# Two attention blocks on one core: where the softmax sums are inverted, and when the next job's sums are formed

## The chip, the cores and the metric

The kernel runs on one core of one Trainium2 chip. The metric is the time of one execution on the device in microseconds (us).

## The reference

The input x has 8 images of 512 channels and 32 x 32 positions (S = 1024 tokens). Two layers follow each other. Each normalises x in 8 groups of channels, projects it to q, k and v (1 x 1 convolutions, 512 to 512 each), runs attention with 8 heads of 64 channels, projects the output and adds x:

```python
xn = ((xg - mean) * jax.lax.rsqrt(var + EPS)).reshape(B, C, H, W)
...
qkv = jnp.einsum('oc,bchw->bohw', qkv_w, xn) + qkv_b[None, :, None, None]
...
attn = jax.nn.softmax(jnp.einsum('bhds,bhdt->bhst', q, k) * scale, axis=-1)
out = jnp.einsum('bhst,bhdt->bhds', attn, v).reshape(B, C, H, W)
return x + jnp.einsum('oc,bchw->bohw', proj_w, out) + proj_b[None, :, None, None]
```

## The kernel before, in words

**Jobs.** The work is cut into 16 jobs, one for an image and a layer, in the order (image 0, layer 0), (image 1, layer 0), (image 0, layer 1), (image 1, layer 1), then the next two images. For each job there are products for v, k and q and the attention. The output projection of job n is done together with the projections of job n+1. All four projections are done with Strassen-like products: seven products of half blocks in place of eight, in most cases over two levels. The sums and differences of blocks that these need are made on VectorE: `sums` (line 1295, tiles `t` and `xn`) and `deep_steps` (tile `deep`, lines 482 to 488) for the next job's normalised input, `out_combine` (line 452 for part 0) for this job's output, `factor` (lines 162 to 168) for the weights.

**Attention.** A job's attention has 8 groups (4 pairs of heads, 2 halves of the queries) of 8 steps each, so 64 steps numbered i = 0 to 63, with i up to 65 to drain. In each step TensorE makes scores `sc` (line 1099), ScalarE takes the exponential into an `e` tile (line 1104), and two steps later TensorE multiplies it with v into `po` (line 1150). The sums over keys are formed beside this: in the first four steps of a group, two `e` tiles are added by a DMA that accumulates (issued by POOL, line 1127) and the sum is added on VectorE five steps later (line 1130); in the last four steps VectorE adds them (lines 1118 and 1120). The `e` tiles come from a pool of twelve, which also holds the weights `w` fetched for the next products. At the end of a group `take` copies half of `po` on ScalarE (`px`, line 1171) and adds the other half on VectorE (line 1173), and `reduce` sums `acc` over its rows into `r` (line 1185).

**The part that is moved.** After every second group, `reduce` sets up four small functions: `gather` (three `r<-r` DMAs on SP, line 1208), `invert` (sum `lt` line 1212, reciprocal line 1213, transposes line 1224, one DMA `rd<-rt` line 1225 and two `rb<-rd` line 1227), `spread` (only in the last pair of groups, line 1236) and `normalise` (a multiplication of two groups' output by `rb`, line 1242). They are put on a clock that the kernel keeps while it is being written out: each attention step advances it by 1.71 us, each end of a group by another 0.85, each step of a projection by its own amount. `later(delay, fn)` puts `fn` at clock + delay, and `advance` emits what has come due. So `times` are planned delays; they set where in VectorE's instruction order a function stands, and the engines then follow the order and their waits.

**Chores and moves.** The other work beside an attention is put at step numbers by hand. `put(i, fn)` places a chore at step i or the next free one, `move(i, fn)` does the same for loads and stores. Among them are the statistics of the next job's input, `groups` and `factors` of its normalisation (lines 331 to 338 and 349 to 351; `factors` needs `mr`, which comes by a DMA, line 341), four `apply` on ScalarE (line 356), the four `sums`, the `deep_steps` and `out_combine`. In jobs 0 to 3 (`ROUNDS`) there is also a "round": a weight is loaded into a tile with the tag `deep`, its factors are formed and seven blocks are stored (`deep<-round`, line 235). In jobs 0 and 1 (`FIRST`) a raw weight is loaded by `put_first` (`raw`, line 157), its factors are formed and stored (`keep<-raw`, line 173). Round, raw weight and deep sums share one buffer, since the tag `deep` has one.

**Order.** TensorE, ScalarE and VectorE run in the order in which the program is written out (`manual_schedule`). The order on SP and POOL is chosen by the planner of the language, by program position and by what it takes to be ready; in the profile the stores of a round stand on SP well ahead of the step at which they are written.

**The end.** The last job has no next one. Its groups go by halves of the queries, and after it `last_proj` makes the output projection in two halves; `put5` (line 1058) and `put` (line 1064) add to x, and the sums for the second half (`last_sums(1)`, lines 1018 to 1027) are placed on the clock from 7.1 us after the attention.

Of the kernel before, what the change touches and what calls it, by code (L numbers as in the profile page):

```python
# [54 lines left out]
ROUNDS = {0: (O, 0), 1: (V, 1), 2: (O, 1), 3: (V, 0)}  # L55
# [26 lines left out]
def fast_path(  # L82
# [33 lines left out]
    def later(delay, fn):  # L116
        todo.append((clock[0] + delay, fn))
# [36 lines left out]
    def load_blocks(w, layer, which):  # L154
        for i in range(2):
            for j in range(2):
                nc.sync.dma_start(w[:, 2 * j + i], raw_block(layer, which, i, j))
# [12 lines left out]
    def store_factors(w, layer, which):  # L170
        keep = wdram.tile([P, NW, 2, CH], F32, name=f"keep_{which}_{layer}")
        for s in (slice(S1, NW), slice(S3, S3 + 1)):
            nc.sync.dma_start(keep[:, s], w[:, s])
        factors[which, layer] = keep
# [272 lines left out]
    def out_combine(src, t, part):  # L447

        b11, b12 = src[:, 0:2, :HALF], src[:, 0:2, HALF:]
        b21, b22 = src[:, 2:4, :HALF], src[:, 2:4, HALF:]  # L450
        if part == 0:
            nc.vector.tensor_sub(b12, b12, b11)
        elif part == 1:
            nc.vector.tensor_sub(t[:, 1], b22, b12)
        elif part == 2:
            nc.vector.tensor_sub(t[:, 0], t[:, 1], b11)
        else:
            nc.vector.tensor_sub(t[:, 2], b21, t[:, 1])
# [619 lines left out]
    class Attention:  # L1078
# [101 lines left out]
        def reduce(self, g):  # L1180
            n, q, m = self.n, self.q, g % 2
            hp, sh = self.groups[g]
            if m == 0:
                self.r = small.tile([P, NQ, 2, RP], F32, tag="r", name=f"r_{n}_{g}", bufs=1)
            nc.vector.tensor_reduce(  # L1185
                self.r[:, 0, m, :], self.acc.pop(g).rearrange("p j (b e) -> p (j b) e", e=RP), AX.X,
                ALU.add, apply_transpose=True,
            )
            if m == 0:
                return  # L1190
            before = self.groups[g - 1]
            if before[0] == hp:
                place = q[:, hp, :].rearrange("p (m e) -> p m e", m=2)
            else:
                place = q[:, hp - 1 : hp + 1, sh * HALF : (sh + 1) * HALF]
            r, first = self.r, slice(0, RP)
            ends = g + 1 == len(self.groups)
            lt = small.tile([RP, 2, RP], F32, tag="lt", name=f"lt_{n}_{g}", bufs=1)
            ri = small.tile([P, 2, 2, RP // 2], F32, tag="ri", name=f"ri_{n}_{g}", bufs=1)
            box = []  # L1200

            def gather():
                for i in range(1, NQ):
                    src, to_ = r[i * RP : (i + 1) * RP, 0], r[first, i]
                    if ends:
                        nc.vector.tensor_copy(to_, src)
                    else:
                        nc.sync.dma_start(to_, src)

            def invert():  # L1210
                inv = ri[first].rearrange("p m j b -> p m (j b)")
                nc.vector.tensor_reduce(lt, r[first].rearrange("p a m b -> p m b a"), AX.X, ALU.add)
                nc.vector.reciprocal(inv, lt)
                box.append(apool.tile([P, 2, HALF], F32, tag="rb", name=f"rb_{n}_{g}", bufs=1))
                if ends:
                    for i in range(1, NQ):
                        nc.vector.tensor_copy(
                            ri[i * RP : (i + 1) * RP, :, 0, :], ri[first, :, i * RP // HD, :]
                        )
                else:  # L1220
                    rt = small.tile([RP, 2, RP], F32, tag="rt", name=f"rt_{n}_{g}", bufs=1)
                    rd = dram.tile([2, 2, HALF], F32, tag="rd", name=f"rd_{n}_{g}")
                    for i in range(2):
                        nc.vector.transpose(rt[:, i, :], inv[:, i, :])
                    nc.sync.dma_start(rd.rearrange("m j (b e) -> (j b) m e", e=RP), rt)
                    for j in range(2):
                        nc.sync.dma_start(
                            box[0][j * HD : (j + 1) * HD],
                            rd[:, j, :].unsqueeze(0).to_broadcast([HD, 2, HALF]),
                        )  # L1230
                nc.vector.tensor_max(lmax, lmax, lt)
                nc.vector.tensor_max(rmax, rmax, inv)

            def spread():
                if ends:
                    nc.vector.transpose(
                        box[0].rearrange("p m (b e) -> p m b e", e=RP),
                        ri[:, :, 0, :].unsqueeze(3).to_broadcast([P, 2, RP // 2, RP]),
                    )

            def normalise():
                nc.vector.tensor_mul(place, place, box[0])
                whole[0] = n if ends else -1

            times = (0.0, 7.6, 7.7, 16.2)
            if ends:
                times = (0.0, 0.2, 7.6, 8.2) if n + 1 >= DEEP_V else (0.0, 0.2, 2.0, 4.0)
                if n + 1 == len(jobs):
                    times = (0.0, 0.2, 2.0, 7.0)
            for at, step in zip(times, (gather, invert, spread, normalise)):  # L1250
                later(at, step)

# [287 lines left out]
    for n in range(-1, len(jobs)):  # L1540
        last = n + 1 == len(jobs)
        outs = None
        if n >= 0:
            chores, moves = {}, {}

            def put(i, fn):
                while i in chores:
                    i += 1
                chores[i] = fn
                return i  # L1550

            def move(i, fn):
                while i in moves:
                    i += 1
                moves[i] = fn
                return i
# [12 lines left out]
                    at = move(at + 1 + i % 2, fn)  # L1569

            def put_first(which, layer):
                at = move(37 if n == 0 else 3, lambda: start()) + 3
                box = []

                def start():
                    box.append(acts.tile([P, NW, 2, CH], F32, tag="deep", name=f"raw_{n}"))
                    load_blocks(box[0], layer, which)

                for part in range(4):
                    at = put(at + 1, lambda part=part: factor(box[0], part))  # L1580
                move(at + 1, lambda: store_factors(box[0], layer, which))

            if last:
                w = last_weights(n)
                for part in range(4):
                    put(12 + 2 * part, lambda part=part: factor(w, part))
                for i, fn in enumerate(last_sums(0)):
                    put(49 + 3 * i, fn)
            else:
                for i, (_, fn) in enumerate(extra):  # L1590
                    put(2 + i, fn)
                if n == 1:
                    at = (8, 14, 15, 16, 18, 19, 21, 24, 27, 30)
                else:
                    for i, fn in zip((3, 3, 4, 5, 5, 6, 7, 7, 8), reads):
                        put(i, fn)
                    at = (16, 22, 23, 24, 26, 27, 29, 31, 33, 35)
                    if n < DEEP_V + 2:
                        at = (17, 23, 24, 25, 27, 28, 30, 32, 34, 36)
                for i, fn in zip(at, steps):  # L1600
                    put(i, fn)
                if n == 1:
                    put_first(*FIRST[n])
                if n in ROUNDS:
                    put_round(*ROUNDS[n])
                if n == 0:
                    put_first(*FIRST[n])
                for i, fn in zip(at[len(steps) :], sums(n + 1)):
                    put(i, fn)
                put(48, lambda q=att.q: out_combine(q, None, 0))  # L1610
                deep_first = deep_steps(n + 1)
                if n + 1 >= DEEP_V:
                    for i, fn in enumerate(deep_first):
                        put((42 if n in ROUNDS else 37) + 2 * i, fn)
                else:
                    for at, fn in zip((50, 52, 54, 56), deep_first[4:]):
                        put(at, fn)
                move(58, lambda: extend_plan(n + 1))
                for _ in range(RING):
                    move(58, fetch)  # L1620
            assert max([*chores, *moves], default=0) < NT * len(att.groups) + LEAD
            if n + 1 >= DEEP_V and not last:
# [17 lines left out]
                att = Attention(n + 1)  # L1640
# [40 lines left out]
        att = Attention(n + 1)  # L1681
# [253 lines left out]
```

## Time and profile before

| | |
|---|---|
| Time, median of 3 runs (lowest to highest) | 3183.94 us (3182.21 to 3186.64) |
| The profiled execution's own time | 3187.94 us |
| Its span in the profile | 3186.2 us |
| Mean granted TensorE clock | 0.996 |
| Busy: TensorE / VectorE / ScalarE / GpSimd | 3156.2 / 2637.2 / 2333.5 / 281.0 us |
| VectorE's waits at L1212 (`lt`, for `r<-r`) | 23.8 us, 20 times |
| VectorE's waits at L1242 (`q`, for `rb<-rd`) | 22.1 us, 11 times |

PE is TensorE's matrix product, PEld its load of weights, DVE VectorE, ACT ScalarE, POOL GpSimd, and SP the engine that issues most transfers. A name such as `lt<-r` gives what an instruction writes and reads. Busy time is the union of an engine's instructions; sequencer work, such as waiting and issuing transfers, is not in it. A number in brackets after an instruction is the engine's idle time ahead of it, and the arrow names what ended it. The ends of TensorE's products are modelled, so a busy TensorE isn't one at its peak; its holes are the part that can be read with certainty.

### The profile page before, as it was taken

What the parts mean: (1) busy time and instruction counts of PE and PEld (TensorE: products, weight loads), DVE (VectorE), ACT (ScalarE), POOL (GpSimd) and SP (SyncE); (2) the same over time, 40 slices, a digit from 0 to 9 for tenths busy, and PEclk for the clock granted to TensorE, in tenths of its full rate; (3) what the DMA queues carried; (4) which work ended last, traced back from release to release, by engine and by line L of the source; (5) the groups of instructions that cost most, each with busy time, mean ns of one, the idle gap of its engine ahead of it and who ended that gap; (6) DMA issues with size and microseconds to landing.
All of it is one profiled execution on the core that took longest, in us unless ns stands there. A gap on an engine that the chain in (4) does not pass through costs nothing.

```text
span 3186.2 us, 62139 instructions
## 1 busy us (share of the span) xinstructions
PE 3156.2 (99%) x24093; PEld 1872.4 (59%) x24093; DVE 2637.2 (83%) x3571; ACT 2333.5 (73%) x4233; POOL 281.0 (9%) x318
## 2 busy tenths in 40 slices
PE   9999999999999999999999999999999999999998
PEld 8357384573846638466393754837557375573844
DVE  8797898978879788797978969889697887978867
ACT  6648687786877868777686776867768687686863
POOL 0101101011010010100001000010000100001000
PEclk9999999999999999999999999999999999999999
DMA  7645675565745455355554545446456463544633
GB/s 276 141 124 160 153 210 140 147 192 128 213 98 146 119 110 167 75 151 159 144 184 88 159 98 138 125 94 181 131 137 182 89 201 63 136 121 96 220 78 78
DMA packets 186190, 450.31 MB, mean 141 GB/s; under 512 B 37928, under 2 KB 54176, under 8 KB 185888
## 3 DMA queue, kind: packets, MB, share of 16 engines
q1 hardware_dynamic: 137040, 296.82, 27.4%
q0 software_dynamic: 48848, 149.44, 25.8%
q8 instruction: 192, 3.15, 0.4%
q14 instruction: 110, 0.90, 0.1%
HBM read 247.41 MB, written 48.17 MB: 93 GB/s over the span
## 4 chain that ended last, share of the span: by engine, by line
PE 81%; DVE 1%; issue 0%; DMA 0%; ACT 0%; SPq 0%; POOL 0%; DVEq 0%; ACTq 0%; POOLq 0%
PE sc L1099 23%; PE po L1150 23%; PE zd L806 9%; PE vd L806 9%; PE yd L806 4%; PE ud L806 4%; PE vd L801 4%; PE zd L801 3%; PE yd L801 1%; PE ud L801 1%; DVE acc L1120 0%; PE z_last L1042 0%; DMA r<-r 0%; ACT e L1104 0%; DVE x L1064 0%
## 5 line engine op out<-in xcount | busy, mean ns | idle before, releaser
L1104 ACT ACTIVATE e<-sc 128x1024 f32<-128x1024 f32 x1024 | 1043.8, 1025 | 575.6 <-PE sc L1099 546.9
L1099 PE MATMUL sc<-q,k 64*64 64x512 f32 x8192 | 1059.2, 590 | 10.1 <-ACT e L1104 10.1
L1150 PE MATMUL po<-e,v 64*64 64x512 f32 x8192 | 1058.0, 590 | 3.4 <-ACT e L1104 3.4
L1099 PEld LDWEIGHTS sc<-q,k 64*64 64x64 f32 x8192 | 309.6, 133 | 576.7 <-issue 509.9
L1150 PEld LDWEIGHTS po<-e,v 64*64 64x64 f32 x8192 | 311.6, 133 | 572.6 <-issue 544.2
L1120 DVE TENSOR_TENSOR acc<-acc,e 128x1024 f32<-128x1024 f32 x320 | 389.4, 1217 | 39.1 <-ACT e L1104 28.9
L1127 POOL DMA_DIRECT2D e<-e x224 | 192.9, 861 | 1769.0 <-ACT e L1104 1267.8
L1118 DVE TENSOR_TENSOR acc<-e,e 128x1024 f32<-128x1024 f32 x128 | 156.4, 1222 | 147.1 <-ACT e L1104 147.1
L1130 DVE TENSOR_TENSOR acc<-acc,e 128x1024 f32<-128x1024 f32 x224 | 272.4, 1216 | 1.9
L806 PE MATMUL zd<-deep,w 128*128 128x256 f32 x860 | 240.2, 379 | 0.0
L806 PE MATMUL vd<-deep,w 128*128 128x256 f32 x804 | 223.4, 379 | 0.0
L806 PEld LDWEIGHTS zd<-deep,w 128*128 128x128 f32 x860 | 163.3, 190 | 22.5 <-ACT ud L501 0.3
L806 PEld LDWEIGHTS vd<-deep,w 128*128 128x128 f32 x804 | 152.8, 190 | 20.8
L1185 DVE TRANSPOSE_TENSOR_REDUCE r<-acc 128x32 f32<-128x1024 f32 x128 | 159.4, 1245 | 4.3
L901 POOL DMA_DIRECT2D x<-p x61 | 72.9, 1195 | 972.9 <-ACT p L823 453.9
L848 DVE TENSOR_TENSOR p<-p,s 128x512 f32<-128x512 f32 x185 | 127.2, 687 | 22.8 <-ACT p L823 19.3
L801 PE MATMUL vd<-w,deep 128*128 128x128 f32 x840 | 119.1, 275 | 1.1 <-ACT ud L501 1.1
L848 DVE TENSOR_TENSOR q<-q,s 128x512 f32<-128x512 f32 x64 | 44.1, 690 | 86.8 <-ACT q L825 45.1
L801 PE MATMUL zd<-w,deep 128*128 128x128 f32 x728 | 106.5, 275 | 0.9 <-ACT ud L501 0.9
L801 PEld LDWEIGHTS vd<-w,deep 128*128 128x128 f32 x840 | 106.2, 192 | 1.3 <-ACT ud L501 1.3
L806 PE MATMUL vd<-os,w 128*128 128x256 f32 x364 | 105.5, 379 | 0.0
L806 PE MATMUL zd<-os,w 128*128 128x256 f32 x356 | 98.9, 379 | 0.0
(296 smaller groups left out, 4826.4 us busy)
## 6 DMA issues: line engine op xcount, KB each, us to landing
w<-deep SPq DMA_DIRECT2D x399, 448.0 KB, 5.4
e<-e POOLq DMA_DIRECT2D x224, 512.0 KB, 4.7
x<-p POOLq DMA_DIRECT2D x61, 512.0 KB, 6.6
rb<-rd SPq DMA_DIRECT2D x96, 256.0 KB, 3.7
x<-x_dram SPq DMA_DIRECT2D x28, 512.0 KB, 3.7
out_dram<-x SPq DMA_DIRECT2D x28, 512.0 KB, 6.0
deep<-w SPq DMA_DIRECT2D x28, 448.0 KB, 2.7
deep<-round SPq DMA_DIRECT2D x28, 448.0 KB, 4.9
```

What stands on the lines that cost most here:

```text
L801: nc.tensor.matmul(ps[:, tokens], moving[i][:, tokens], lhs[:, FACTOR[i], :], start=(start and ti == 0), stop=True, skip_group_check=True,)
L806: nc.tensor.matmul(ps, lhs[:, FACTOR[i], :], moving[i], start=start, stop=True, skip_group_check=True,)
L848: nc.vector.tensor_add(to_, to_, five.to_broadcast([P, 2, QT]))
L901: nc.gpsimd.dma_start(to_, p(part), accum_op=ALU.add)
L1099: nc.tensor.matmul(sc[h * HD : (h + 1) * HD, j, :], k[r, hp, k0 : k0 + HD], q[r, hp, sh * HALF : (sh + 1) * HALF], start=True, stop=True,)
L1104: nc.scalar.activation(e, sc, AF.Exp, scale=SCALE)
L1118: nc.vector.tensor_add(acc[g], self.es[i - 1], e)
L1120: nc.vector.tensor_add(acc[g], acc[g], e)
L1127: nc.gpsimd.dma_start(self.summed[i], self.summed.pop(i - 1), accum_op=ALU.add)
L1130: nc.vector.tensor_add(self.acc[g], self.acc[g], self.summed.pop(i))
L1150: nc.tensor.matmul(po[g][j * HD : (j + 1) * HD, h, :], v[r, kc, d0 : d0 + HD], e[r, j, :], start=(kc == 0), stop=(kc == NT - 1),)
L1185: nc.vector.tensor_reduce(self.r[:, 0, m, :], self.acc.pop(g).rearrange("p j (b e) -> p (j b) e", e=RP), AX.X, ALU.add, apply_transpose=True,)
```

## The change

In jobs 0 to 3 and groups 0 to 3, the planned delays of `invert` and `normalise` go from 7.6 to 12.0 and from 16.2 to 22.0 us. In the last pair of groups of the last job, `normalise` goes from 7.0 to 9.6. In job 0 the load of the raw weight is asked for at move 31 instead of 37, and by the rule for taken slots stands at 33 (37 before); the four factors follow at steps 37 to 40 (41 to 44 before) and the store at 41 (45 before). Part 0 of `out_combine` goes from step 48 to 52 in jobs 0 to 3. The eight deep sums of jobs 1 to 3 go from 42, 44, 46, 49, 50, 52, 54, 56 to 39, 40, 41, 43, 45, 47, 49, 50; the four of job 0 from 50, 52, 54, 56 to 46 to 49. All other jobs keep their places.

```diff
-            times = (0.0, 7.6, 7.7, 16.2)
+            times = (0.0, 12.0, 12.1, 22.0) if n in ROUNDS and g < 4 else (0.0, 7.6, 7.7, 16.2)
             if ends:
                 times = (0.0, 0.2, 7.6, 8.2) if n + 1 >= DEEP_V else (0.0, 0.2, 2.0, 4.0)
                 if n + 1 == len(jobs):
-                    times = (0.0, 0.2, 2.0, 7.0)
+                    times = (0.0, 0.2, 2.0, 9.6)
...
             def put_first(which, layer):
-                at = move(37 if n == 0 else 3, lambda: start()) + 3
+                at = move(31 if n == 0 else 3, lambda: start()) + 3
...
-                put(48, lambda q=att.q: out_combine(q, None, 0))
+                put(52 if n in ROUNDS else 48, lambda q=att.q: out_combine(q, None, 0))
                 deep_first = deep_steps(n + 1)
                 if n + 1 >= DEEP_V:
                     for i, fn in enumerate(deep_first):
-                        put((42 if n in ROUNDS else 37) + 2 * i, fn)
+                        put(37 + 2 * i if n not in ROUNDS else (39, 40, 41, 43, 45, 47, 49, 50)[i], fn)
                 else:
-                    for at, fn in zip((50, 52, 54, 56), deep_first[4:]):
+                    for at, fn in zip((46, 47, 48, 49), deep_first[4:]):
                         put(at, fn)
```

## The prediction

> **What bounds it now.** I read the engines' shares first, then busy time in 50 us stretches, then the waits and the timeline around each TensorE hole.
>
> ```profile
> PE 3156.2 (99%) x24093; PEld 1872.4 (59%) x24093; DVE 2637.2 (83%) x3571; ACT 2333.5 (73%) x4233; POOL 281.0 (9%) x318
> ...
> 100.00:150.00 50.00, 46.64 (x424) 15.87 (x420) 28.72 (x42) 32.20 (x34) 7.89 (x9) 0.97 0.72 171
> 150.00:200.00 50.00, 46.40 (x427) 15.58 (x420) 46.28 (x55) 28.62 (x30) 3.94 (x5) 1.00 0.49 115
> ...
> 500.00:550.00 50.00, 46.42 (x432) 16.17 (x428) 40.44 (x56) 32.66 (x35) 7.43 (x8) 1.00 0.64 156
> ...
> 700.00:750.00 50.00, 46.81 (x424) 16.15 (x420) 40.41 (x56) 32.36 (x34) 7.42 (x8) 0.97 0.63 152
> ...
> 900.00:950.00 50.00, 50.00 (x472) 17.74 (x468) 39.23 (x53) 35.71 (x38) 6.57 (x8) 1.00 0.48 93
> ```
>
> The columns are stretch, length, then PE, PEld, DVE, ACT and POOL busy. TensorE sets the pace and is full nearly everywhere; no work on it is removed. Only its holes can be won, 3186.2 − 3156.2 = 30 us in all, and about 7 of those are the last output's way out. The holes lie in jobs 0 to 3, the jobs that the change touches. In job 3:
>
> ```profile
> 730.38 1.22 DVE L1120 TENSOR_TENSOR acc<-acc,e 128x1024 f32<-128x1024 f32 x1
> 733.54 0.59 DVE L1212 TENSOR_REDUCE lt<-r 32x64 f32<-32x256 f32 x1 [1.94 <-DMA r<-r]
> ...
> 736.34 0.14 DVE L349 TENSOR_TENSOR mul<-mr,vec_sb 128x4 f32<-128x4 f32 x1
> ...
> 736.91 1.24 ACT L356 ACTIVATE xn<-x,off,mul 128x1024 f32<-128x1024 f32 x1 [4.19 <-DVE off L351]
> ...
> 739.11 1.99 PE L1099 MATMUL sc<-q,k 64*64 64x512 f32 x8 [3.19 <-ACT e L1104]
> ```
>
> The chain is: `invert` of the second group (L1212) waits for its row sums; behind it on VectorE stand the next job's `factors` (L349 to L351); ScalarE's `apply` (L356) waits for those; behind it stands the next exponential, and TensorE runs out of score buffers. Job 0 shows the same (3.36 us at 125) and job 2 too (3.00 at 536, 0.58 at 541). Job 1 does not: its `factors` come at step 14, ahead of `invert`. Later holes are VectorE arriving late:
>
> ```profile
> 146.70 1.23 DVE L1242 TENSOR_TENSOR q<-q,rb 128x1024 f32<-128x1024 f32 x1 [14.70 <-DMA rb<-rd]
> ...
> 197.87 1.09 PE L1150 MATMUL po<-e,v 64*64 64x512 f32 x8 [3.36 <-ACT e L1104]
> ...
> 209.06 2.53 PE L553 MATMUL v<-w,t 128*128 128x256 f32 x7 [2.77 <-DVE q L1173]
> ...
> 416.16 1.16 PE L801 MATMUL zd<-w,deep 128*128 128x128 f32 x8 [0.86 <-ACT ud L501]
> ...
> 420.64 0.71 PE L801 MATMUL vd<-w,deep 128*128 128x128 f32 x4 [1.09 <-ACT ud L501]
> ...
> 3164.93 1.99 PE L1042 MATMUL z_last<-t_last,w_last 128*128 128x256 f32 x8 [1.34 <-DVE x L1064]
> ```
>
> In job 0 `normalise` (L1242) holds VectorE idle for 14.7 us. From then to 217 VectorE has almost no gap (44.98 busy of 48.78 us to 195.5), so it never catches up: TensorE stops twice, 6.1 us. In job 1 the backlog appears in the next job's products, 1.95 us.
>
> **What the skill says.** The Trainium skill, "PSUM — Partial Sum Buffer", Engine vs sequencer instructions, calls the ScalarE, VectorE and GpSimdE queues strict FIFO. The trace agrees: `factors` start 0.1 us after the add behind the delayed `invert`. "DMA: Bandwidth & Descriptors", Queues, rings and completion order, has each DMA engine take one queue's descriptors in ring order; here the 8 KB `r<-r` transfers have a median of 3.7 us to landing, far over what their size needs. Its Anatomy section gives about 2.0 us fixed per DMA, an estimate of the floor that later issue can't remove; `rd<-rt` shows 2.0.
>
> **The change, part by part.** Nothing is added or removed: the same VectorE instructions and the same DMAs, at other places. A step is about 1.72 us.
>
> *Invert and multiplication, groups 1 and 3 of jobs 0 to 3.* By the kernel's clock `invert` moves from the end of step 22 (38) into step 25 (41), `normalise` from the end of 26 (42) to that of 30 (46). `factors` at step 23 then precede `invert` in jobs 0, 2 and 3. In job 3 the next add needs an exponential done at 732.7 at the latest; it starts at 731.6 and ends at 732.8, `factors` take 0.45, so ScalarE waits some 0.6 us instead of 4.19. The unknown is `mr<-dg`, issued ahead of `r<-r` (725.6 against 727.7; median landing 2.2 us, thus near 730). At worst it lands with `r`, and `factors` start at 733.5: a ScalarE wait of 1.3 us. The two-deep score buffer covered 4.2 − 3.2 = 1 us, so the hole would be 0.3. I take 3.36 (job 0), 3.4 (job 2) and 3.1 (job 3). ScalarE then has four `apply` (1.24 each) and a copy (0.58) in six steps that leave 0.69 each; job 4 carries the same without a hole. I charge 0.8 in all for small new holes (0 to 3).
>
> *Behind the later invert* stand that step's `apply` on ScalarE (independent), then the paired add and the row reduction. Each `rd` and two `rb` DMAs follow it on SP. In jobs 2 and 3 the seven stores `deep<-round` now go ahead of them: `rb` then lands near 545 in job 2 (issue 540.5, median 3.7), while VectorE, after step 30's add and sum, is ready near 546. POOL is passed by nothing.
>
> *Rest of job 0.* `r` is ready before, but `rb` depends on SP: the stores end at 131, then
>
> ```profile
> 131.17 0.38 SPq L157 DMA_DIRECT2D raw<-wqkv_dram  x1
> 131.61 0.46 SPq L1225 DMA_DIRECT2D rd<-rt  x1
> 132.11 1.45 SPq L157 DMA_DIRECT2D raw<-wqkv_dram  x3
> 134.16 2.26 SPq L1227 DMA_DIRECT2D rb<-rd  x2
> ```
>
> Here `rt`, written at 124.3, waited 7.3 us behind `raw`, which waits for the stores out of its buffer. Asking for `raw` at step 33 instead of 37 can't bring it before 131, but a later `rd` will stand behind all four `raw` (1 MB): +2 us. Against this the paired-sum transfers, which landed at 141.2 and 146.2 in the same jam, start 3.4 us sooner. I put the landing at 144 (142 to 150; it was 146.7). Four steps' work (adds 1.15 + 1.2, first sum 1.16 = 3.5 us) now runs ahead of this wait instead of behind it. The second wait, 2.86 us at 173.9, comes back larger: only 5.7 us of work lies between `invert` and `normalise` (6.7 before), and the store of `raw` (1 MB) now runs ahead of `rd`; I take 4.0 (0 to 6). VectorE ends 3.5 + 2.7 − 1.2 = 5.0 us sooner. The raw block's four differences (0.62 each, steps 37 to 40 for 41 to 44) and the transposed sums (0.9 each, 46 to 49 for 50 to 56) only change places in this backlog; the first of these sums needs the store of `raw` to have left the buffer, some 7 us after issue at about 161, when VectorE gets there at about 168: a wait of up to 2 us that runs inside the one for `rb`. The holes sum to 9.5 in job 0 and shrink by that much: 5.0, of which 3.36 is counted, leaving 1.6 (−2.4 to 6.1).
>
> *Next job's sums sooner, output's difference later.* This reorders a saturated VectorE and makes no time by itself. My count by step in jobs 2 and 3 (adds 1.2, reduction 1.25, sums 1.14 and 0.9) gives a peak backlog of 3.6 us at steps 42 and 50, against 3.0 and 2.5; the twelve exponential buffers carried ten steps in job 0, so nothing stops. In job 1 the waits of 0.25 and 1.58 us at L1212 vanish, and the 1.95 us of holes with them; I take 1.7. The first sum at step 39 needs the stores out of the same buffer: issued by 353 in job 1 with the step at 360, and 540 against 562 in job 2.
>
> *Last normalisation.* It moves behind the four additions L1064 that free `z_last`. TensorE's 1.34 us wait loses the 1.2 us of L1242, less rounding: 1.1. The sums after it are needed no sooner than it leaves them.
>
> Sum: 3.36 + 3.4 + 3.1 + 1.6 + 1.7 + 1.1 − 0.8 = **13.5 us**. The profiled execution took 3187.9, which gives 3174.4. It stands 4.0 above the median of 3183.9 (highest 3186.6); some of these DMA waits are likely shorter in an ordinary run, so I take 12.4 there: **3171.5 us**.
>
> **Rivals.** *The wait moves, it doesn't go.* With `factors` freed, VectorE stands at `normalise` or at `mr` instead, and job 0 gives nothing beyond its first hole. For it: L1242 already waited 11 times, 22.1 us. Against: five extra steps until `rb` is read in most rounds. Gain 13.5 − 1.6 − 2.4 − 2 = 7.5, time 3177 (up to 3180 if job 1's 1.7 and a little more are lost too).
>
> *Nothing measurable.* The holes are mostly the profiled execution's own (it is the slowest seen), or new ones at steps 39 to 50 repay them: 3178 to 3189.
>
> *Slower: `rb` of job 0.* Behind `raw` it lands so late that exponential buffers run out. At 146.7 TensorE will be at step 38 with about ten of twelve in use, so from about 149 each us is a TensorE us. The other parts give 9.3 net of new holes, and job 0 must lose that: it decides from about 159, slower beyond 166; at 168 some 3191. For it: the saturated DMA share there (over 1.0 at 136 to 144). Against: only 1.5 MB lie ahead.
>
> **Numbers.** Forecast 0.74, its own range 3164.5 to 3175; the wait moves 0.12; nothing measurable 0.09; slower 0.05. About 0.2% (6.4 us) is what a measurement tells from no change. The moved wait falls a little short of it at its upper end (0.02), which gives faster 0.84, same 0.11, slower 0.05. Lowest: all holes go, 9.5 + 1.95 + 3.58 + 3.19 + 1.34 = 19.6. Highest: a gain of about 4. Range 3164.5 to 3179.5.
>
> **What would show it.** Right: no L1212 wait in jobs 0 to 3; `factors` directly behind an add; no TensorE hole near 125, 533 and 730; the last `z_last` hole under 0.3. Job 0: L1242's first wait under 11 us. Wrong: L1242 or L349 waits where L1212 did, holes at steps 39 to 50 of jobs 1 to 3, or a job 0 whose holes exceed 6 us.

## The result, and the profile after

The changed kernel takes 3176.45 us (median of 18 runs, 3172.03 to 3180.97), the kernel before 3184.15 us beside it (18 runs, 3179.16 to 3188.1): 7.7 us less, a ratio of 0.9974 with a 95% interval of 0.9968 to 0.9981. The profiled execution after took 3175.27 us with a span of 3173.5, 12.7 us less than the profiled one before.

The engines' shares on the page, and four of the same 50 us stretches as before (stretch, length, then PE, PEld, DVE, ACT, POOL busy, then the granted TensorE clock, the DMA share and GB/s):

```profile
PE 3153.8 (99%) x24093; PEld 1875.1 (59%) x24093; DVE 2635.5 (83%) x3571; ACT 2330.9 (73%) x4233; POOL 280.9 (9%) x318
...
100.00:150.00 50.00, 50.00 (x472) 17.67 (x468) 31.19 (x44) 34.79 (x36) 8.45 (x9) 1.00 0.73 181
150.00:200.00 50.00, 45.21 (x396) 16.87 (x389) 47.76 (x57) 26.30 (x28) 3.48 (x4) 0.96 0.47 119
500.00:550.00 50.00, 49.47 (x464) 17.40 (x460) 39.97 (x54) 35.59 (x37) 7.43 (x8) 1.00 0.60 148
700.00:750.00 50.00, 49.47 (x468) 17.33 (x462) 40.77 (x53) 34.78 (x36) 8.28 (x9) 1.00 0.63 153
```

The instructions are the same in number. TensorE's idle time (span less busy) fell from 30.0 to 19.7 us, and its busy time by 2.4 us. The first holes of jobs 0, 2 and 3 are closed but for half a microsecond; the stretch from 150 to 200 in job 0 isn't. Job 3 around step 25, from the timelines of VectorE, ScalarE and TensorE (start, us, what, idle before and its end):

```profile
722.40 2.55 DVE L1120 TENSOR_TENSOR acc<-acc,e 128x1024 f32<-128x1024 f32 x2
724.86 0.15 DVE L349 TENSOR_TENSOR mul<-mr,vec_sb 128x4 f32<-128x4 f32 x1
...
728.71 0.58 DVE L1212 TENSOR_REDUCE lt<-r 32x64 f32<-32x256 f32 x1
...
725.45 1.24 ACT L356 ACTIVATE xn<-x,off,mul 128x1024 f32<-128x1024 f32 x1 [0.71 <-DVE off L351]
...
730.18 1.09 PE L1099 MATMUL sc<-q,k 64*64 64x512 f32 x8 [0.53 <-ACT e L1104]
```

`factors` (L349) follow an add at once, ScalarE waits 0.71 us for them where it waited 4.19, and `invert` (L1212) waits for nothing. Part of the wait has gone elsewhere: over the run VectorE's waits at L1212 fell from 23.8 to 14.7 us, and those at L1242 rose from 22.1 to 29.2. VectorE, ScalarE and TensorE in job 2:

```profile
539.69 1.22 DVE L423 TENSOR_TENSOR t<-xn 128x1024 f32<-128x1024 f32 x1
544.08 1.23 DVE L1242 TENSOR_TENSOR q<-q,rb 128x1024 f32<-128x1024 f32 x1 [3.17 <-DMA rb<-rd]
...
611.03 0.37 ACT L829 COPY s<-zd 128x256 f32<-128x256 f32 x1 [2.37 <-DVE v L844]
...
612.01 0.71 PE L801 MATMUL vd<-w,deep 128*128 128x128 f32 x4 [1.08 <-ACT ud L501]
```

`normalise` now waits 3.17 us for `rb` where it waited for nothing, and 67 us later, in the next job's products, ScalarE waits for VectorE and TensorE for ScalarE: a hole of 1.08 us that was not there before. Job 3 has the same (waits of 2.38 and 2.21, holes of 0.34 and 1.09). And in job 0, VectorE, ScalarE and TensorE, with the last hole of the run below them:

```profile
149.04 1.23 DVE L1242 TENSOR_TENSOR q<-q,rb 128x1024 f32<-128x1024 f32 x1 [12.51 <-DMA rb<-rd]
...
152.76 1.94 ACT L1104 ACTIVATE e<-sc 128x1024 f32<-128x1024 f32 x2 [3.77 <-DVE acc L1130]
...
153.84 1.09 PE L1099 MATMUL sc<-q,k 64*64 64x512 f32 x8 [1.71 <-ACT e L1104]
...
194.57 1.09 PE L1150 MATMUL po<-e,v 64*64 64x512 f32 x8 [1.88 <-ACT e L1104]
...
3153.94 1.99 PE L1042 MATMUL z_last<-t_last,w_last 128*128 128x256 f32 x8 [0.20 <-DVE x L1064]
```

While VectorE waits 12.51 us for `rb`, the additions behind it wait too. An exponential then waits 3.77 us for one of them (L1130), which gives an `e` buffer free, and TensorE stops for 1.71 us at a place where it didn't stop before. The hole of 1.34 us ahead of the last `z_last` product is down to 0.20.

The table is worked out from the traces, for all kernels told of below. A job's time runs from the start of its first exponential (L1104) to that of the next job's; jobs 4 to 14 take 195.6 each in every kernel, but for four single jobs of 195.9 to 196.6. The end is from the start of the last exponential of the run to the end of the span. Holes are TensorE gaps over 0.3 us. The columns from job 0 on are one profiled execution each.

| kernel | median us | ratio to before, 95% | job 0 | job 1 | job 2 | job 3 | end | holes |
|---|---|---|---|---|---|---|---|---|
| before | 3184.15 | | 213.2 | 198.0 | 199.6 | 200.6 | 35.6 | 20.9 |
| after | 3176.45 | 0.9974 (0.9968 to 0.9981) | 207.0 | 196.7 | 197.9 | 198.8 | 32.8 | 12.2 |
| before again | 3185.51 | 1.0003 (0.9995 to 1.0012) | 211.2 | 198.4 | 200.5 | 199.7 | 36.0 | 21.0 |
| times only | 3177.15 | 0.9972 (0.9961 to 0.9982) | 206.8 | 196.1 | 200.5 | 198.1 | 36.0 | 15.3 |
| chores only | 3182.24 | 0.9991 (0.9983 to 1.0000) | 210.9 | 196.6 | 199.8 | 200.6 | 35.8 | 18.0 |
| tail only | 3182.43 | 0.9996 (0.9988 to 1.0005) | 208.0 | 197.4 | 201.7 | 199.8 | 34.6 | 15.4 |
| normalise later | 3165.68 | 0.9937 (0.9924 to 0.9951) | 203.6 | 196.4 | 196.3 | 196.3 | 33.0 | 6.5 |
| invert sooner | 3173.25 | 0.9962 (0.9948 to 0.9976) | 208.4 | 196.4 | 196.7 | 196.9 | 34.6 | 10.5 |
| rb on POOL | 3167.41 | 0.9943 (0.9930 to 0.9957) | 200.4 | 200.3 | 196.6 | 196.3 | 32.8 | 7.8 |
| raw late | 3176.81 | 0.9976 (0.9967 to 0.9985) | 207.9 | 196.9 | 197.4 | 198.2 | 33.1 | 11.0 |
| later and POOL | 3166.87 | 0.9943 (0.9930 to 0.9957) | 202.1 | 195.9 | 196.3 | 196.3 | 34.9 | 5.3 |
| later, old sums | 3170.33 | 0.9953 (0.9939 to 0.9966) | 208.1 | 196.0 | 196.3 | 196.3 | 33.2 | 9.0 |
| later, invert back | 3176.17 | 0.9974 (0.9962 to 0.9985) | 203.2 | 196.5 | 201.0 | 200.9 | 33.1 | 12.9 |

Each ratio is to runs of the kernel before on the same chip, whose medians were 3184.15, 3185.02, 3185.36 and 3184.85 us; differences between medians of different rows can be off by about 1 us for this alone. A kernel has 5 to 18 runs. Single executions differ most in job 0: "before", "before again" and "tail only" have the same code up to the last job, and job 0 takes 213.2, 211.2 and 208.0.

**What a hole costs.** The traces also record the clock that TensorE was granted. Between the start-up and the end of a run it falls to half in stretches of 3.41 or 6.83 us, and each of these begins within 2 us of the end of a hole. Two holes of nearly the same length in the profile before, the 3.00 us of job 2 and the 3.19 us of job 3, differ in this (busy time and clock in the 3.3 to 3.4 us behind each; the columns are as above):

```profile
539.30:542.70 3.40, 2.81 (x24) 0.87 (x28) 2.90 (x3) 3.40 (x5) 0.86 (x1) 1.00 1.05 317
739.10:742.40 3.30, 3.29 (x16) 1.05 (x20) 2.80 (x3) 3.30 (x5) 0.00 (x0) 0.50 1.04 306
```

Of the fifteen holes of 2.96 to 3.39 us at step 25, in the five traces that have them, eleven came with such a stretch and four did not; what decides it is not shown. In jobs 2 and 3 a job with such a hole took 199.6 to 199.8 us where the clock stayed full and 200.5 to 201.7 where it fell. If the holes and half of the time at half clock are taken off a job's time, 195.3 to 196.8 us are left for jobs 1 to 3 in all thirteen traces, and 197.9 to 199.2 for job 0. So these two terms account for the differences between the jobs of the table to about 1.5 us, and a hole can cost 1.7 to 3.4 us of clock beside its own length.

### The profile page after: what moved, and what is told of

The parts are those of the page before. It is cut to its first block, busy times and chain, and to the rows that moved or that the text cites. A ratio compares the mean times of both kernels' runs of the same rounds, so it can differ in the third digit from the quotient of the medians.

```text
span 3173.5 us, 62149 instructions
## 1 busy us (share of the span) xinstructions
PE 3153.8 (99%) x24093; PEld 1875.1 (59%) x24093; DVE 2635.5 (83%) x3571; ACT 2330.9 (73%) x4233; POOL 280.9 (9%) x318
## 4 chain that ended last, share of the span: by engine, by line
PE 90%; DVE 5%; DMA 2%; issue 1%; SPq 0%; ACT 0%; DVEq 0%; POOL 0%; ACTq 0%; POOLq 0%
PE sc L1099 24%; PE po L1150 24%; PE vd L806 11%; PE zd L806 11%; PE yd L806 5%; PE ud L806 4%; PE vd L801 4%; PE zd L801 3%; DVE acc L1120 1%; PE ud L801 1%; PE yd L801 1%; DMA rb<-rd 1%; PE z L553 1%; DMA rd<-rt 1%; DVE acc L1130 1%
## 5 line engine op out<-in xcount | busy, mean ns | idle before, releaser
L1104 ACT ACTIVATE e<-sc 128x1024 f32<-128x1024 f32 x1024 | 1043.5, 1025 | 575.1 <-PE sc L1099 546.9
L1130 DVE TENSOR_TENSOR acc<-acc,e 128x1024 f32<-128x1024 f32 x224 | 272.6, 1217 | 1.7
L1242 DVE TENSOR_TENSOR q<-q,rb 128x1024 f32<-128x1024 f32 x64 | 77.4, 1209 | 29.9 <-DMA rb<-rd 29.2
```

Source lines behind the costliest of these rows:

```text
L1104: nc.scalar.activation(e, sc, AF.Exp, scale=SCALE)
L1130: nc.vector.tensor_add(self.acc[g], self.acc[g], self.summed.pop(i))
```

## The experiments

**Before again.** No edit.

> The kernel before, unchanged, as a control of one profiled execution against another. If the profile before was a slow draw, this one is near 3184 us, its TensorE holes over 0.3 us sum to clearly less than the 19.7 us seen there, and the missing part is in job 0 (14.7 us wait at L1242, holes at 194 and 206). If the profile was typical and the timed runs hide less, the holes again sum to 19 to 20 us at 3184 us.

3185.51 us, and this profiled execution took 3185.80. The holes again sum to 21.0 us (20.9 in the first profile), with the same three at step 25 (3.35, 2.96, 3.07) and VectorE's 14.0 us wait at L1242. So the holes belong to the kernel and not to one execution; neither branch of the expectation holds whole, since the holes stay and the time is below the first profile's 3187.94. Job 0's late holes vary in place: 1.12, 0.59 and 4.10 here against 3.36 and 2.77.

**Times only.** The kernel before, with one line of the change:

```diff
-            times = (0.0, 7.6, 7.7, 16.2)
+            times = (0.0, 12.0, 12.1, 22.0) if n in ROUNDS and g < 4 else (0.0, 7.6, 7.7, 16.2)
```

> Only the planned delays of invert and normalise in groups 0 to 3 of jobs 0 to 3 are changed. My theory (factors no longer queue behind the wait at L1212): the holes at step 25 of jobs 0, 2 and 3 are gone, and this alone gives most of the change, 5 to 7 us of the 7.7 us. Rival (the earlier deep sums are what makes room on VectorE): at most 3 us here, because the waits only move to L1242 and VectorE is late at the end of jobs 0 to 3.

3177.15 us: 7.9 us less than before, so this line by itself gives as much as the whole change. Of the holes at step 25 the one of job 0 is gone and 0.53 us each is left in jobs 2 and 3, as the theory has it. The rival's wait is there too, 3.24 and 1.55 us at L1242 in job 2, and job 2 is no shorter than before:

```profile
542.52 1.23 DVE L1242 TENSOR_TENSOR q<-q,rb 128x1024 f32<-128x1024 f32 x1 [3.24 <-DMA rb<-rd]
```

**Chores only.** The change without its two lines of `times`.

```diff
-                at = move(37 if n == 0 else 3, lambda: start()) + 3
+                at = move(31 if n == 0 else 3, lambda: start()) + 3
...
-                put(48, lambda q=att.q: out_combine(q, None, 0))
+                put(52 if n in ROUNDS else 48, lambda q=att.q: out_combine(q, None, 0))
...
-                        put((42 if n in ROUNDS else 37) + 2 * i, fn)
+                        put(37 + 2 * i if n not in ROUNDS else (39, 40, 41, 43, 45, 47, 49, 50)[i], fn)
...
-                    for at, fn in zip((50, 52, 54, 56), deep_first[4:]):
+                    for at, fn in zip((46, 47, 48, 49), deep_first[4:]):
```

> The raw load at 31, out_combine's part 0 at 52 and the earlier deep sums, with the planned delays of before and the last normalisation where it was. My theory: within 2 us of before, the holes at step 25 stay (about 3 us in jobs 0, 2 and 3). Rival (the order of the sums is what matters): 4 us or more faster, and the holes at the end of jobs 0 and 1 are gone.

3182.24 us, 2.8 less than before, a little over the 2 us expected, with an interval that just includes no change. The three holes at step 25 stay (3.35, 3.08, 3.19). Job 1 is 1.4 us shorter. The rival's 4 us are not there, and holes at the end of jobs 0 and 1 remain (2.10 and 1.81, and 0.73).

**Tail only.** The kernel before, with the last normalisation at 9.6 instead of 7.0.

```diff
-                    times = (0.0, 0.2, 2.0, 7.0)
+                    times = (0.0, 0.2, 2.0, 9.6)
```

> Only the last normalisation is later. My theory: the hole of 1.34 us ahead of the last z_last product shrinks to about 0.2 us and the time falls by 1.1 us. Rival (the end is set by the last output's landing): no change in the time from the last exponential to the end of the span.

The hole ahead of `z_last` is gone, and the last product starts 26.89 us after the last exponential instead of 28.05: 1.16 us. How much of it reaches the end varies: with this edit the end is 32.8 to 34.9 us in nine profiles, without it 35.6 to 36.0 in four. The median fell by 2.6 us, with an interval that includes no change. Taken alone, the three parts save 7.9, 2.8 and 2.6 us, and together 7.7: that the last two add anything to the first isn't shown.

**Normalise later.** The kernel after, one number.

```diff
-            times = (0.0, 12.0, 12.1, 22.0) if n in ROUNDS and g < 4 else (0.0, 7.6, 7.7, 16.2)
+            times = (0.0, 12.0, 12.1, 25.5) if n in ROUNDS and g < 4 else (0.0, 7.6, 7.7, 16.2)
```

> The kernel after, with the planned delay of normalise in groups 0 to 3 of jobs 0 to 3 at 25.5 us instead of 22.0 (end of step 32 and 48 instead of 30 and 46). If VectorE's waits at L1242 (3.2 us in job 2, 2.4 and 2.2 in job 3, 12.5 in job 0) are what makes it late at the end of these jobs, they shrink by 3.4 us each, the holes of 1.1 us in the next products vanish, and it is 2 to 4 us faster than the kernel after. Rival (the holes at the end come from the amount of VectorE work alone): the waits shrink and the holes stay, same time as after.

3165.68 us, 10.8 less than the kernel after, where 2 to 4 were expected. The waits at L1242 in jobs 1 to 3 are gone and so are the holes at the end of jobs 2 and 3. VectorE in job 2:

```profile
538.36 1.22 DVE L425 TENSOR_TENSOR t<-xn,t 128x1024 f32<-128x1024 f32 x1
539.49 1.22 DVE L1242 TENSOR_TENSOR q<-q,rb 128x1024 f32<-128x1024 f32 x1
540.63 0.68 DVE L1173 TENSOR_TENSOR q<-po,px 128x512 f32<-128x512 f32 x1
```

Nothing is idle around L1242. Both jobs take 196.3 us, 0.7 from the 195.6 of the undisturbed ones. The amount of VectorE work is the same, so in jobs 2 and 3 the rival falls: it was the waits. In job 0 the wait fell from 12.5 to 9.0 us, and a hole of 3.32 is left at 196. Part of what is beyond the expectation lies in the clock: over all runs the mean granted clock is 0.9992 here and 0.9979 in the kernel after, which is about 4 us of 3170.

**Invert sooner.** The kernel after, with 10.2 and 10.3 in place of 12.0 and 12.1.

> The kernel after, with invert at 10.2 us instead of 12.0, so that it stands directly behind factors at the end of step 23 and not in step 25. If the lateness of rb is set by when invert writes it out, the waits at L1242 fall by about 3 us in jobs 2 and 3 and it is 1 to 3 us faster than after. Rival (rb is held by the stores and the raw loads ahead of it on SP): the same waits at L1242 as after within 1 us, and the same time.

3173.25 us. L1242 waits 2.04 us in job 2 and 2.47 in job 3, hardly less than after (3.17 and 2.38), but the second wait of job 3 and that of job 1 are gone, and job 2 and job 3 are 1.2 and 1.9 us shorter. Neither expectation holds whole. SP in job 2, and for this kernel VectorE, show why the first wait there stays; the kernel after, then this one:

```profile
529.85 2.23 SPq L235 DMA_DIRECT2D deep<-round  x2
532.29 0.91 SPq L1225 DMA_DIRECT2D rd<-rt  x1
538.33 1.87 SPq L1227 DMA_DIRECT2D rb<-rd  x2
```

```profile
525.91 4.52 SPq L235 DMA_DIRECT2D deep<-round  x5
530.53 1.04 SPq L1225 DMA_DIRECT2D rd<-rt  x1
531.62 1.06 SPq L235 DMA_DIRECT2D deep<-round  x1
533.99 2.07 SPq L1227 DMA_DIRECT2D rb<-rd  x2
...
542.64 1.23 DVE L1242 TENSOR_TENSOR q<-q,rb 128x1024 f32<-128x1024 f32 x1 [2.04 <-DMA rb<-rd]
```

`invert` has written `rt` by 528.6 here and by 532.3 in the kernel after, 3.7 us sooner. But `rd` (8 KB) stands behind six of the seven stores of 448 KB and is issued only 1.8 us sooner. `rb` can be issued when `rd` has landed, 3.5 us after its issue here and 6.0 in the kernel after; then it lands 8.6 us after its own first issue here and 5.7 there. The two together take 12.1 and 11.8 us, so the sooner `invert` wins little.

**rb on POOL.** The kernel after, with those transfers on another queue.

```diff
-                    nc.sync.dma_start(rd.rearrange("m j (b e) -> (j b) m e", e=RP), rt)
+                    (nc.gpsimd if n in ROUNDS and g < 4 else nc.sync).dma_start(rd.rearrange("m j (b e) -> (j b) m e", e=RP), rt)
...
-                        nc.sync.dma_start(
+                        (nc.gpsimd if n in ROUNDS and g < 4 else nc.sync).dma_start(
```

> The kernel after, with the DMAs rd and rb of groups 1 and 3 of jobs 0 to 3 issued by POOL instead of SP. If SP's order (raw loads and stores ahead) is what makes rb late, job 0's first wait at L1242 falls from 12.5 us to under 6 and its holes (5.2 us) mostly go: 3 to 5 us faster than after. Rival (the transfers themselves are slow, since the sixteen DMA engines are full): the wait stays over 9 us. A side effect to look for: POOL waits for rd ahead of the paired-sum transfers, which would then be late.

3167.41 us. VectorE and POOL in job 0, and ScalarE in job 1:

```profile
138.94 1.23 DVE L1242 TENSOR_TENSOR q<-q,rb 128x1024 f32<-128x1024 f32 x1 [4.07 <-DMA rb<-rd]
```

```profile
126.53 0.60 POOL L1225 DMA_DIRECT2D rd<-rt  x1 [9.11 <-DVE rmax L1232]
131.08 1.20 POOL L1227 DMA_DIRECT2D rb<-rd  x2 [3.95 <-DMA rd<-rt]
132.27 1.90 POOL L1127 DMA_DIRECT2D e<-e  x2
```

```profile
346.58 1.94 ACT L1104 ACTIVATE e<-sc 128x1024 f32<-128x1024 f32 x2 [2.65 <-DMA e<-e]
```

Job 0's wait is 4.1 us instead of 12.5, so SP's order was most of it, and the job is 6.6 us shorter: `rd` is issued 45.7 us into the job, and 53.0 in the kernel after, where it stands behind the four `raw` loads. The side effect is there as well: POOL stands for 3.95 us until `rd` has landed, and the paired sums `e<-e` go out late. In job 1, where less was to be gained (2.17 us), TensorE has a new hole of 1.72 us at 346 behind an exponential, and the job is 3.6 us longer. The trace has the exponential wait 2.65 us for such a sum; no run tried this alone.

**Raw late.** The kernel after, with the raw load at 37 again (`move(37 if n == 0 else 3, ...)`).

> The kernel after, with the raw load of job 0 asked for at 37 again. If asking sooner puts the store of raw ahead of the second rd and delays VectorE, job 0 is 1 to 2 us shorter than after. Rival (the sooner load makes room for the sums): job 0 is 1 to 3 us longer, with the holes at its end back.

3176.81 us and 207.9 us for job 0, against 3176.45 and 207.0: no difference that can be told. Neither expectation is borne out: the sooner load has no effect that shows.

**Later and POOL.** Normalise at 25.5, and `rd` and `rb` on POOL in job 0 alone (`n == 0 and g < 4`).

> The kernel after with normalise at 25.5 us in groups 0 to 3 of jobs 0 to 3, and in job 0 alone rd and rb of groups 1 and 3 issued by POOL. If the two causes are separate (rb late for normalise in all four jobs; SP's raw load ahead of rb in job 0), job 0 takes about 200 us as with rb on POOL and jobs 1 to 3 about 196.3 each as with normalise later: 3161 to 3163 us. Rival (both remove the same wait): as with normalise later alone, 3165 to 3166 us.

3166.87 us, the rival's number: no better than normalise later alone (3165.68; the intervals overlap). In the trace job 0 is 1.5 us shorter and the end 1.9 us longer. There is no wait at L1242 left in job 0, but a hole of 1.88 us at 198 stays, with two of half a microsecond; what makes VectorE late there is not shown.

**Later, old sums.** Normalise at 25.5, with the deep sums where they were before the change (the last two pairs of lines under "Chores only" undone).

> The kernel after with normalise at 25.5 us in groups 0 to 3 of jobs 0 to 3, but with the deep sums where they were before (42, 44 and so on in jobs 1 to 3; 50, 52 and so on in job 0). If the sooner sums only reorder a full VectorE, the time is that with normalise later alone, 3165.7, within 1.5 us. Rival (they clear the end of the attention): 2 us or more slower, with holes in the first products after jobs 1 to 3.

3170.33 us, 4.7 slower than with the sooner sums. In the traces it is all in job 0, 208.1 against 203.6, where TensorE waits at the end of the attention:

```profile
202.19 2.07 PE L553 MATMUL v<-w,t 128*128 128x256 f32 x4 [4.57 <-DVE q L1173]
```

Jobs 1 to 3 are the same to 0.4 us. So the sooner sums do matter, but only in job 0: there the second `normalise` waits 3.30 us for `rb`, and with three of the sums ahead of it (0.95 us each) it waits for nothing.

**Later, invert back.** Normalise at 25.5, with `invert` at 7.6 as before.

> The kernel after with normalise at 25.5 us in groups 0 to 3 of jobs 0 to 3, but with invert at 7.6 us as before. If the holes at step 25 come from factors behind the wait at L1212, they are back in jobs 0, 2 and 3 (3.0 to 3.4 us each) and it is 8 to 10 us slower than with normalise later alone, some 3174 to 3176 us. Rival (the later normalise alone made the gain): within 2 us of 3165.7.

3176.17 us, 10.5 slower than with `invert` late. The holes at step 25 are back; TensorE in job 2:

```profile
528.45 1.09 PE L1099 MATMUL sc<-q,k 64*64 64x512 f32 x8 [3.01 <-ACT e L1104]
```

Jobs 0 and 3 have 3.35 and 3.17. Nothing waits over 0.1 us at L1242 in jobs 0 to 3, so these holes are from `factors` behind L1212 alone. What they cost is in jobs 2 and 3, 4.7 and 4.6 us. Job 0 is no longer than with `invert` late (203.2 against 203.6): with `invert` back `rd` is issued at 132.2 and has landed by 135.0, with it late at 134.4 and by 140.8, and the wait of 9.02 us and the hole of 3.32 that follow take back what the freed `factors` gave.

## Why the prediction was right, and where it was off

It is faster, as forecast, by 7.7 us where 12.4 were forecast. 3176.5 lies in the range (3164.5 to 3179.5), but just above the forecast case's own (to 3175) and next to the first rival's 3177. The direction came from the stated cause; the size is nearer to that rival's, whose moved wait the traces show. Of the signs named, these came: no L1212 wait in jobs 0 to 3, `factors` directly behind an add, the last hole under 0.3. Holes of 0.53 us are left at 532 and 730, job 0's first wait is 12.5 us and not under 11, and L1242 waits where L1212 did, which was named as a sign of being wrong. Step by step:

**`factors` freed: right.** Forecast 3.36, 3.4 and 3.1 us of holes won in jobs 0, 2 and 3; measured 3.36, 3.05 and 2.66 (what is left are holes of 0.53 behind the four `apply`). The run with `invert` back shows the cause in jobs 2 and 3, and the `mr` transfer was in time. In job 0 the hole goes too, but that run shows no gain in the job's time. (A slip of reading: in the profile before, `factors` begin as the add of 735.20 ends, not 0.1 us after it; the order is as stated.)

**Behind the later invert: the step that failed.** I put `rb` of job 2 near 545 and VectorE near 546. Job 2 starts 6.3 us sooner than it did, so these are 538.7 and 539.7 on the new trace; measured were 544.1 and 540.9. The term that was mis-sized is the landing of `rd` and then `rb`: I took the medians of the whole run, 2.0 and 3.7 us, 5.7 in all. Behind the stores it took 11.8 (6.0 and 5.7). In job 2 of other kernels it was 11.9 (times only, 3.1 and 8.7), 12.1 (invert sooner) and 10.5 (raw late, 3.1 and 7.4): the split varies, and the sum is about twice what I took. The 2.0 us were no floor either: the Anatomy section of the Trainium skill's "DMA: Bandwidth & Descriptors" gives them for transfers issued by GpSimd, and `rd`, which SP issues, landed within 1.4 us in job 1 of the profile before. The first rival, the wait that moves to `normalise`, came true to that extent. VectorE has no room to make up 3.17 us before the job ends, so the loss comes out as holes in the next products: jobs 2 and 3 gave 1.7 and 1.8 us instead of 3.4 and 3.1. With `normalise` later both are there (3.3 and 4.3).

**Job 0: direction right, sizes off.** `rb` landed at 149.0 instead of 144, and the second wait was 1.58 us instead of 4.0. The errors partly cancel: the holes after the first sum to 5.2 us against 6.1 before, 0.9 won where 1.6 were forecast. The hole of 1.71 us at 152 is new; it is what the rival "slower" described, exponential buffers that run out because `rb` is late, on a small scale.

**Sums: a reordering, as said, with one exception.** I gave their moves no time of their own. Jobs 2 and 3 bear that out; job 0 doesn't, 4.5 us there once `normalise` is at 25.5, where the sums fill VectorE's time ahead of a wait. Job 1: forecast 1.7, measured 1.3.

**Last normalisation: right in the trace.** Forecast 1.1; the last product comes 1.14 us sooner. That the median falls by it isn't shown.

**A term left out: the clock behind a hole.** I counted a hole at its own length. The lines that I showed have a clock of 0.97 in two of the 50 us stretches with a hole, which is 1.5 us each, and I gave it nothing. In jobs 0 to 3 the half clock costs 6.8 us in the profile before and 3.4 in the one after.

**From the profile to the median: too small a correction.** The sum of 13.5 against the profiled execution was near (12.7), but by luck: the errors cancel. Job 0 gave 6.2 us instead of 5.0, job 1 gave 1.3 instead of 1.7, jobs 2 and 3 gave 3.5 instead of 6.5, the end 2.8 instead of 1.1, and job 0 began 1.2 us later, where I had charged 0.8 for new holes. I took 1.1 us off for an ordinary run; 5.0 were due: the profile before stands 3.8 above its median, the profile after 1.2 below. My reason, shorter waits in ordinary runs, is not borne out: the second profile of the kernel before, close to its median, has the same holes. The spread of single executions (9 us from lowest to highest in both kernels) is of the size of the whole effect. Part of it is whether the clock falls behind a hole (in jobs 0 to 3 it took 6.8 us in the first profile of the kernel before and 5.1 in the second); the rest stays open.

## What to carry to other kernels

On an in-order engine, a wait costs by what stands behind it: moving three small instructions (`factors`, 0.45 us) ahead of a wait of 1.9 us closed all but 0.5 us of a hole of 3.2 us on another engine. Count such a hole at its length and at what the clock behind it may take. But moving the start of a chain of transfers later moves its end as well, so move the consumer by more than the producer; here 3.5 us more for `normalise` was worth more than the whole change. Price a chain of transfers by its landings in a stretch with the same load and not by the medians of the run, and compare medians with medians, since a profile is one execution.

## What was not expected of the hardware

Holes of about 3 us drew a half clock of 3.41 us in ten of fifteen cases and of 6.83 us in one more, with the same code drawing it in one execution and not in the next.

A chain of an 8 KB transfer and two of 256 KB that read it took 10.5 to 12.1 us behind stores of 448 KB on the same queue (job 2, four kernels), where the medians of the profile before sum to 5.7. Its first part alone is no fixed price: behind the seven stores the 8 KB took 6.0 us in the kernel after and 3.1 in five others. From POOL's queue, with the same stores just issued on SP, the chain took 10.0 us in job 2 (4.9 for its first part). So in job 2, where `rd` was issued from SP without delay in the kernel after, another queue won little; in job 0 it won much, because there SP stood still until the stores had left the buffer that `raw` needs.
